# Two transformer blocks: attention scores as three float32r products of high and low halves instead of one fp32 product

## The chip, the cores and the metric

The kernel is one program on one core of a Trainium2 chip. The profile shows five engines: TensorE (PE for its matmuls, PEld for its weight loads), VectorE (DVE), ScalarE (ACT), GpSimd (POOL) and SyncE (SP), which here does nothing but issue DMAs. The metric is device time in microseconds (us) from the first to the last instruction, as the median of several runs. The profile and the trace come from one profiled execution; durations of single instructions below are from it.

## The reference

Two blocks (layers 0 and 1), each of them self-attention, cross-attention and a gated feed-forward, on x of 4 batches x 512 tokens x 320 features, with a context of 4 x 1601 x 192:

```python
def _attn(x, ctx, wq, wk, wv, wo, bo, heads):
    b, n, _ = x.shape
    j = ctx.shape[1]
    dh = wq.shape[1] // heads
    scale = dh ** (-0.5)
    q = (x @ wq).reshape(b, n, heads, dh).transpose(0, 2, 1, 3)
    k = (ctx @ wk).reshape(b, j, heads, dh).transpose(0, 2, 1, 3)
    v = (ctx @ wv).reshape(b, j, heads, dh).transpose(0, 2, 1, 3)
    sim = jnp.einsum('bhid,bhjd->bhij', q, k) * scale
    a = jax.nn.softmax(sim, axis=-1)
    out = jnp.einsum('bhij,bhjd->bhid', a, v)
    out = out.transpose(0, 2, 1, 3).reshape(b, n, heads * dh)
    return out @ wo + bo
h1 = _ln(x, n1_g, n1_b)
x = _attn(h1, h1, q1, k1, v1, o1_w, o1_b, heads) + x
h2 = _ln(x, n2_g, n2_b)
x = _attn(h2, context, q2, k2, v2, o2_w, o2_b, heads) + x
h3 = _ln(x, n3_g, n3_b)
proj = h3 @ ff_w1 + ff_b1
a, g = jnp.split(proj, 2, axis=-1)
ff = a * jax.nn.gelu(g, approximate=False) @ ff_w2 + ff_b2
return ff + x
```

There are 20 heads of 16 features. Everything is fp32.

## The kernel before

**Units.** The work is a list of units (class `Unit`, line 271). An attention unit is one layer, one batch and one group of four heads; there are five groups, so 20 self units, then 20 cross units, then 4 feed-forward units, and all of it again for layer 1. A self unit has 512 keys in `nch` = 4 chunks of 128, a cross unit 1601 keys in 13 chunks, the last of them with 65. Each of the four heads has its own 32 rows ("slot") of the tiles `q` and `kT`: 16 rows of features and one row that carries minus the row maximum (in `q`) against ones (in `kT`), the others zero.

**A chunk.** `main` (line 1068) goes over the chunks c of a unit. For a chunk it emits two rounds (`round_of`, line 1062) and a value product. A round is two score products (`score`, line 1072: keys by queries, 128 x 512 into one bank of `ps_st`), for heads 0 and 1 or for heads 2 and 3, and, from the iterator `pair` that `give` hands out, the score products for the maxima of the other two heads of a later unit (`full_two`, line 903: queries by keys, into a double bank of `ps_m`). Thus all four slots have a matmul in every round. After the matmuls come the exponentials (ACT, line 1083, into a tile of the pool `prs`) and one maximum over 128 x 2 x 512 (DVE, line 922). The value product of the chunk before follows (`values`, line 1090, four matmuls into `ps_st`), is copied by ACT into a tile `vo` of `prs` (line 1113), and added to `o` by POOL (line 1114). PSUM has four single banks for scores, values and projections (`ps_st`) and two double banks for maxima (`ps_m`).

**Maxima come first.** The score products of a unit need the maxima of its rows, so these run a unit or two ahead. `max_pairs` (line 886) makes two queues of maxima: one for heads 2 and 3, one for heads 0 and 1, each with 4 entries in a self unit and 13 in a cross unit (12 of full width and one for the last 65 keys). `give` (line 1329) hands out one entry for each round if the coming unit is `at_hand` (line 1303: its queries and keys have been in place for at least three rounds); and when the unit's start comes near (`rest == 1`, line 1344) it makes whatever is left into extra rounds without scores, which take one entry of each queue: four heads, two reductions. After a unit's last maxima, two chunks before the unit ends, `max_end` (line 966) transposes the maxima on DVE and moves them into the rows of `q` by eight DMAs on SP.

**The planner.** All else (normalisation, queries and keys, values, the output projection) waits in chains (`chains`, line 329) with costs and due times. `steps` (line 398), called once for each chunk, runs those that are due, and lets the chain "slots" run one entry for each call (`clock["slots"]`). `queries` and `keys` (lines 693, 719) project, copy the bank by ACT to a stage, and let POOL write the stage into the slots (`to_slots`, line 632). `keys_of_context` (line 747), for cross units, has four entries in "slots" instead, each of which moves one head's rows by three DMAs (`piece`, line 767); after the last one `kwhen` is set, on which `at_hand` looks.

All instructions of an engine run in the order in which this program emits them. The two lines that the text below returns to most:

```python
return not (v.q is None or v.kwhen is None) and clock["round"] >= max(v.qwhen, v.kwhen) + 3
clock["slots"] -= name == "slots"
```

## Time and profile before

| what | value |
|---|---|
| median of 3 runs (lowest to highest) | 3195.73 us (3195.3 to 3197.33) |
| the profiled execution: its span | 3195.3 us |
| PE busy | 3163.1 us (99%), granted clock 0.998 on the mean |
| DVE busy | 2069.2 us (65%) |
| ACT busy | 1972.4 us (62%) |
| POOL busy | 1204.1 us (38%) |
| first to last chunk of self units, layer 0 and layer 1 | 369.0 and 370.5 us (79 chunks each) |
| the 19 cross units behind them | 888.4 and 877.9 us (247 chunks each) |

The span of the profiled execution lies within 0.02% of the median, so it is used as the time before. The last two rows are differences between the copies of the value products (lines 1108 and 1113) in the trace, of which there is one for each chunk. Busy time is the union of an engine's or a group's instructions. A group of the list of lines names its source line, engine, operation, output<-inputs and shapes, how many there were, the busy time, the mean of one in ns, and the idle time of the engine before them with what ended it. An fp32 matmul leaves two records in the trace, each with a weight load of its own.

### The profile page before, as it was taken

How to read it: one execution, taken by the hardware profiler on the slowest of the kernel's cores; microseconds unless marked ns; L12 is line 12 of the kernel's file. 1: busy time of each engine (PE TensorE's matmuls, PEld its weight loads, DVE VectorE, ACT ScalarE, POOL GpSimd, SP SyncE). 2: the span in 40 equal slices, each digit the busy share in tenths (PEclk: the TensorE clock that was granted, in tenths of full speed). 3: DMA queues.
4: the chain of work that ended last, by engine and by line, in shares of the span. 5: the costliest groups of instructions: out<-in, count | busy, mean ns of one | idle time of the engine just before them, and what ended most of it. 6: DMA issues, size and time to landing. Idle time of an engine off the chain costs nothing. (4 is left out here: it accounts for less than half of the span.)

```text
span 3195.3 us, 81370 instructions
## 1 busy us (share of the span) xinstructions
PE 3163.1 (99%) x33970; PEld 1466.6 (46%) x33970; DVE 2069.2 (65%) x2662; ACT 1972.4 (62%) x3951; POOL 1204.1 (38%) x1617
## 2 busy tenths in 40 slices
PE   9999999999999999999999999999999999999999
PEld 4444444444444444355444444444444444443555
DVE  7787777778678677422247777777777777773221
ACT  4666577777777777611147665777778777785110
POOL 5555334443443443301135553344434444432000
PEclk9999999999999999999999999999999999999999
DMA  2220011100100100100012100010010010001000
GB/s 67 56 70 17 14 26 39 33 21 19 33 21 20 33 16 11 39 6 0 1 30 61 34 14 14 22 28 16 16 32 10 16 33 9 16 11 37 9 11 15
DMA packets 104851, 77.84 MB, mean 24 GB/s; under 512 B 42908, under 2 KB 95012, under 8 KB 104484
## 3 DMA queue, kind: packets, MB, share of 16 engines
q1 hardware_dynamic: 104400, 72.63, 9.3%
q8 instruction: 268, 4.39, 0.6%
q14 instruction: 99, 0.81, 0.1%
q0 software_dynamic: 64, 0.00, 0.0%
q10 hardware_dynamic: 20, 0.00, 0.0%
HBM read 33.04 MB, written 7.93 MB: 13 GB/s over the span
## 5 line engine op out<-in xcount | busy, mean ns | idle before, releaser
L1083 ACT ACTIVATE pr<-st 128x512 f32<-128x512 f32 (+1 forms) x2720 | 1408.6, 602 | 420.7 <-PE sps L906 360.4
L1077 PE MATMUL st<-q,kT 32*128 32x512 f32 (+1 forms) x5440 | 1362.6, 614 | 2.6 <-DVE nmax L922 1.7
L922 DVE TENSOR_REDUCE pm<-sps 128x2 f32<-128x1024 f32 (+1 forms) x974 | 1134.4, 1203 | 268.9 <-PE sps L906 262.4
L906 PE MATMUL sps<-kT,q 32*128 32x512 f32 x5120 | 1275.7, 621 | 14.2 <-DVE nmax L922 9.8
L1114 POOL TENSOR_TENSOR o<-o,vo 128x512 f32<-128x512 f32 x576 | 734.5, 1275 | 1375.8 <-ACT vo L1113 1200.7
L1077 PEld LDWEIGHTS st<-q,kT 32*128 32x128 f32 (+1 forms) x5440 | 503.8, 181 | 517.4 <-ACT pr L1083 291.1
L1097 PE MATMUL av<-pr,vals 128*32 128x512 f32 (+1 forms) x5440 | 729.3, 605 | 0.3
L922 DVE TENSOR_REDUCE nmax<-sps 128x2 f32<-128x1024 f32 (+1 forms) x338 | 378.5, 1160 | 151.7 <-PE sps L906 149.1
L906 PEld LDWEIGHTS sps<-kT,q 32*128 32x128 f32 x5120 | 406.1, 183 | 125.8 <-issue 80.6
L1113 ACT COPY vo<-av 128x512 f32<-128x512 f32 x576 | 339.8, 590 | 45.2 <-PE av L1097 41.1
L1097 PEld LDWEIGHTS av<-pr,vals 128*32 128x32 f32 (+1 forms) x5440 | 110.0, 108 | 493.4 <-ACT pr L1083 480.2
L1199 PE MATMUL fps<-hT,w 128*128 128x512 f32 x640 | 286.1, 600 | 1.0 <-DVE kT L1223 0.5
L1222 ACT ACTIVATE gl<-fps,b 128x512 f32<-128x512 f32 x80 | 50.7, 684 | 371.0 <-PE fps L1212 268.0
L647 POOL TENSOR_SCALAR q<-qst,keep,zero 64x128 f32<-64x128 f32 (+1 forms) x476 | 232.3, 488 | 58.9 <-ACT qst L711 25.5
L1199 PEld LDWEIGHTS fps<-hT,w 128*128 128x128 f32 x640 | 119.2, 191 | 152.1 <-issue 146.9
L699 PE MATMUL qps<-hT,wq 112*32 112x128 f32 (+3 forms) x2880 | 126.8, 310 | 0.5 <-DVE pm L922 0.5
L1024 PEld LDWEIGHTS ops<-wo,aT 112*32 112x32 f32 (+1 forms) x3072 | 98.4, 110 | 62.2 <-issue 32.5
L1223 DVE SCALAR_TENSOR_TENSOR hid<-fps,b,gl 128x512 f32<-128x512 f32 x48 | 33.8, 746 | 143.0 <-ACT gl L1222 143.0
L438 POOL TENSOR_SCALAR root<-root 128x4 f32<-128x4 f32 x23 | 5.3, 230 | 315.5 <-DVE root L432 314.8
L1024 PE MATMUL ops<-wo,aT 112*32 112x160 f32 (+1 forms) x3072 | 123.9, 299 | 0.2
L699 PEld LDWEIGHTS qps<-hT,wq 112*32 112x32 f32 (+1 forms) x2880 | 86.7, 110 | 79.3 <-issue 38.8
L1260 DVE TENSOR_TENSOR x<-yps,x 128x320 f32<-128x320 f32 x32 | 15.7, 492 | 148.5 <-PE yps L1253 148.5
(88 smaller groups left out, 2255.7 us busy)
## 6 DMA issues: line engine op xcount, KB each, us to landing
kT<-kst SPq DMA_DIRECT2D x320, 48.0 KB
aT<-o SPq DMA_DIRECT2D x320, 32.0 KB
q<-turned SPq DMA_DIRECT2D x636, 1.0 KB
w<-in_L_xattn_ff_w_dram SPq DMA_DIRECT2D x20, 256.0 KB
ctxT<-ctxT SPq DMA_DIRECT2D x24, 208.0 KB
ctxT<-ctxT SPq DMA_DIRECT2D x12, 416.0 KB
ctxin<-in_ctx_dram SPq DMA_DIRECT2D x24, 192.0 KB
w<-in_L_xattn_ff_w_dram SPq DMA_DIRECT2D x20, 160.0 KB
```

The costliest lines, as they stand in the source:

```text
L647: nc.gpsimd.tensor_scalar(to, stage[rows, :w], keep[b][rows], more[rows], ALU.mult, ALU.add)
L699: nc.tensor.matmul(ps[to, :w], lhsT=wq[:n, k, gs], rhs=first.hT[:n, k, at[i] : at[i] + w], start=(k == 0), stop=(k == 2),)
L906: nc.tensor.matmul(ps, lhsT=u.q[j * SLOT : (j + 1) * SLOT, t * P : (t + 1) * P], rhs=u.kT[j * SLOT : (j + 1) * SLOT, u.k0 + s * 512 : u.k0 ...
L922: nc.vector.tensor_reduce(to[:, j : j + n], part, AX.X, ALU.max, negate=(ns == 1))
L1024: nc.tensor.matmul(ps[f : f + m, : D // 2], lhsT=aT[:n, k, t * P + f : t * P + f + m], rhs=wo[:n, k, cols], start=(k == 0), stop=(k == 2),)
L1077: nc.tensor.matmul(st[:r, :], lhsT=u.kT[rows, u.k0 + u.cols[c] : u.k0 + u.cols[c] + r], rhs=u.q[rows, :], start=True, stop=True)
L1083: nc.scalar.activation(p[:r], st[:r], AF.Exp)
L1097: nc.tensor.matmul(ps[i * SLOT : (i + 1) * SLOT, :], lhsT=columns_of[:r, head : head + SLOT], rhs=pr.pop((c, j))[:r, :], start=True, stop= ...
L1113: nc.scalar.copy(vo, ps)
L1114: nc.gpsimd.tensor_tensor(u.o, u.o, vo, ALU.add)
L1199: nc.tensor.matmul(ps, lhsT=w1[:, k, i * FF + c * P : i * FF + (c + 1) * P], rhs=u.hT[:, k, :], start=ahead and k == 0, stop=not ahead and ...
L1222: nc.scalar.activation(gl, pss[1], AF.Gelu, bias=b1[:, NHC + c : NHC + c + 1])
```

## The change

A score is computed from exact sums. Queries and keys are each written as high + low, where high is the value rounded by a write with type float32r and low is the rest. A head's 32 rows of `kT` now hold, for each of 16 features, a high row and a low row; `q` has two halves side by side, the high one and the low one, each with every feature's row twice. A score for a maximum is two float32r matmuls (the high half of q, then the low half, against the same keys); a score for the softmax is these two and a third one of two rows, minus the maximum's high and low part (`mrow`) against ones.

What moves with it:

- `round_of` emits the passes of all products of a round interleaved: first pass of each, second pass of each, third pass.
- The split is done on a stage by POOL, two instructions (`split`); the rows then go to `q` and `kT` by DMAs on SP: for a self unit four for the queries and four for the keys, for a cross unit twice four and six. Each of these DMAs is an entry of the chain "slots", of which `steps` still runs one for each chunk; the marks `qwhen` and `kwhen` are set by the last entry of their group. When a stage is needed again (`stages`, `empty`) or a unit is needed at once (`at_once`), the entries left in a group are run there; their places in the chain stay, and do nothing when their turn comes.
- `max_end` splits the maxima (two more DVE instructions) and writes them by eight DMAs to `mrow`, a tile of its own.
- The pool `prs` has 8 tiles instead of 9, `oturn` one instead of two; wq2 and the stage of the cross keys lie in the room of w2, wv2 in that of w1, the context's input in that of w1r; so w1r and w2 are loaded with w1, in the last cross unit; the last four hidden tiles of the feed-forward are taken from `prs`. The tiles of blanks and their DMAs are gone.

```diff
-    prs = ctx.enter_context(tc.tile_pool(name="prs", bufs=9))
+    prs = ctx.enter_context(tc.tile_pool(name="prs", bufs=8))
...
-    qbuf = [const.tile([P, N], F32, name=f"q{i}") for i in range(4)]
+    qbuf = [const.tile([P, 2, N], F32, name=f"q{i}") for i in range(4)]
+    mrows = [const.tile([P, N], F32, name=f"m{i}") for i in range(2)]
...
-    def to_slots(t, c0, stage, w, i, with_ones, direct=None):
...
+    def split(x, high):
+
+        eng = nc.vector if start["on"] else nc.gpsimd
+        eng.tensor_scalar(high.bitcast(F32R), x, 1.0, None, ALU.mult)
+        eng.tensor_tensor(x, x, high, ALU.subtract)
...
+    groups = {"stage": deque(), "kstage": deque()}
+
+    def empty(kind, left):
+
+        while len(groups[kind]) > left:
+            g = groups[kind].popleft()
+            while g:
+                g.popleft()()
+
+    def stages(kind="stage"):
+        empty(kind, kind == "stage")
+        if kind == "kstage":
+            return [*kstage, None]
+        t = two.tile([P, 2, N // 2], F32, tag="stage", name="stage")
+        return [t[:, e] for e in range(2)] + [t]
+
+    def slots_soon(u, fs, name, kind="stage"):
+
+        fs = list(fs)
+        done = fs.pop()
+
+        def last():
+            done()
+            setattr(u, name, -9 if start["on"] else clock["round"])
+
+        group = deque(fs + [last])
+        groups[kind].append(group)
+        u.slots.append(group)
+        if start["on"]:
+            empty(kind, 0)
+        for _ in tuple(group):
+            add("slots", 0.0, lambda: group and group.popleft()(), clock["round"] + 3, yes, ready_at(clock["round"] + 2))
+
+    def ready_at(r):
+        return lambda: clock["slots"] > 0 and clock["round"] >= r
...
+            high, low, both = stages()
+            nc.scalar.mul(low[:, :w], ps[:, :w], DH**-0.5)
+            split(low[:, :w], high[:, :w])
+
+            def move(s, i):
+                queue = (nc.sync, nc.scalar)[s] if start["on"] else nc.sync
+                queue.dma_start(
+                    out=u.qbuf.rearrange("(r s) e n -> s r e n", s=2)[s][:, :, at[i] : at[i] + w],
+                    in_=both[i * GD : (i + 1) * GD, :, :w],
+                )
+
+            slots_soon(
+                u, [lambda s=s, i=i: move(s, i) for i in range(2) for s in range(2)],
+                "qwhen" if part == parts - 1 else "qpart",
+            )
...
+            slots_soon(u, [lambda e=e, i=i: move(e, i) for e in range(2) for i in range(3)], "kwhen", "kstage")
...
+        def passes(heads, outs, queries, keys):
+
+            def one_pass(e):
+                for j, out in zip(heads, outs):
+                    rows = slice(j * SLOT, (j + 1) * SLOT)
+                    nc.tensor.matmul(
+                        out,
+                        lhsT=u.q[rows, e, queries].bitcast(F32R),
+                        rhs=u.kT[rows, keys].bitcast(F32R),
+                        start=(e == 0),
+                        stop=(e == 1),
+                    )
+
+            return [lambda e=e: one_pass(e) for e in range(2)]
...
+        nc.vector.tensor_scalar(both[:, :n].bitcast(F32R), u.nm, 1.0, None, ALU.mult)
+        nc.vector.tensor_tensor(both[:, n:], u.nm, both[:, :n], ALU.subtract)
+        nc.vector.transpose(turned, both)
+        to = u.mrow.rearrange("(j s) (t i r) -> i s j t r", s=SLOT, t=NQ, r=SLOT)
+        for i in range(P // SLOT):
+            for e in range(2):
+                rows = slice(i * SLOT + e * n, i * SLOT + (e + 1) * n)
+                queue = (nc.sync, nc.scalar)[e] if start["on"] else nc.sync
+                queue.dma_start(out=to[i, e], in_=turned[rows, :])
...
     def round_of(scores, maxima):
 
-        then = [f() for f in scores] + [f() for f in maxima]
-        for f in then:
-            f()
+        todo = [f() for f in scores] + [f() for f in maxima]
+        for i in range(max((len(passes) for passes, _ in todo), default=0)):
+            for passes, _ in todo:
+                if i < len(passes):
+                    passes[i]()
+        for _, then in todo:
+            then()
...
-            nc.tensor.matmul(
-                st[:r, :], lhsT=u.kT[rows, u.k0 + u.cols[c] : u.k0 + u.cols[c] + r], rhs=u.q[rows, :], start=True, stop=True
-            )
+            keys = u.kT[rows, u.k0 + u.cols[c] : u.k0 + u.cols[c] + r].bitcast(F32R)
+            two_rows = slice(j * SLOT, j * SLOT + 2)
+
+            def product(e):
+                nc.tensor.matmul(st[:r, :], lhsT=keys, rhs=u.q[rows, e, :].bitcast(F32R), start=(e == 0), stop=False)
+
+            def less_maximum():
+                nc.tensor.matmul(
+                    st[:r, :],
+                    lhsT=units_of[two_rows, :r].bitcast(F32R),
+                    rhs=u.mrow[two_rows, :].bitcast(F32R),
+                    start=False,
+                    stop=True,
+                )
...
-        return not (v.q is None or v.kwhen is None) and clock["round"] >= max(v.qwhen, v.kwhen) + 3
+        return not (v.qwhen is None or v.kwhen is None) and clock["round"] >= max(v.qwhen, v.kwhen) + 3
...
-        while v.kslots:
-            v.kslots.popleft()()
+        for group in v.slots:
+            while group:
+                group.popleft()()
```

## Prediction

> **What bounds the kernel now.** The page first: PE is busy 99% of the span, and the four groups that a score costs are the largest of their engines.
>
> ```profile
> span 3195.3 us, 81370 instructions
> PE 3163.1 (99%) x33970; PEld 1466.6 (46%) x33970; DVE 2069.2 (65%) x2662; ACT 1972.4 (62%) x3951; POOL 1204.1 (38%) x1617
> ...
> L1083 ACT ACTIVATE pr<-st 128x512 f32<-128x512 f32 (+1 forms) x2720 | 1408.6, 602 | 420.7 <-PE sps L906 360.4
> L1077 PE MATMUL st<-q,kT 32*128 32x512 f32 (+1 forms) x5440 | 1362.6, 614 | 2.6 <-DVE nmax L922 1.7
> L922 DVE TENSOR_REDUCE pm<-sps 128x2 f32<-128x1024 f32 (+1 forms) x974 | 1134.4, 1203 | 268.9 <-PE sps L906 262.4
> L906 PE MATMUL sps<-kT,q 32*128 32x512 f32 x5120 | 1275.7, 621 | 14.2 <-DVE nmax L922 9.8
> ```
>
> ACT and DVE wait for PE (420.7 and 268.9 us), PE for nobody. Next, one chunk in the timeline of cross units (start, length, engine and line):
>
> ```profile
> 1002.78 0.70 PE L1077 MATMUL st<-q,kT 32*128 32x512 f32 x2
> 1002.79 0.70 PE L906 MATMUL sps<-kT,q 32*128 32x512 f32 x2
> 1002.97 0.59 ACT L1113 COPY vo<-av 128x512 f32<-128x512 f32 x1
> ...
> 1003.75 0.59 PE L1077 MATMUL st<-q,kT 32*128 32x512 f32 x2
> ...
> 1003.93 2.06 ACT L1083 ACTIVATE pr<-st 128x512 f32<-128x512 f32 x4 [0.38 <-PE sps L906]
> 1004.04 2.36 DVE L922 TENSOR_REDUCE pm<-sps 128x2 f32<-128x1024 f32 x2 [0.57 <-PE sps L906]
> ...
> 1004.71 1.07 PE L1097 MATMUL av<-pr,vals 128*32 128x512 f32 x8
> ```
>
> Four heads run side by side (starts 10 ns apart), records follow each other every 0.43 us, two to a product. The two rounds take 1004.71 - 1002.78 = 1.93, the value product another 0.98 (to the next round in a chunk without projections): **PE 2.92 us for a chunk**. **ACT needs 2.45**: four exponentials in 2.06 less 0.60 for the last makes 0.49 from one to the next, times five with the copy. **DVE needs 2.34**: two maxima, 1.17 apart. So PE may gain 0.47 us for a chunk before ACT ends it, and only while DVE gets its two maxima in every chunk. The third view, busy time by stage (self and cross units of layer 0, then of layer 1; PE, weight loads, DVE, ACT, POOL):
>
> ```profile
> 43.40:412.40 369.00, 361.42 (x4490) 165.35 (x4498) 285.71 (x393) 237.21 (x483) 182.96 (x279) 1.00 0.16 41
> 412.40:1300.80 888.40, 884.81 (x10858) 402.41 (x10842) 656.98 (x762) 677.12 (x1368) 373.08 (x423) 1.00 0.10 25
> 1639.40:2009.90 370.50, 363.05 (x4536) 165.90 (x4536) 277.58 (x365) 237.80 (x484) 180.15 (x266) 1.00 0.13 32
> 2009.90:2887.70 877.80, 876.84 (x10852) 397.43 (x10836) 644.09 (x720) 675.33 (x1365) 372.68 (x423) 1.00 0.09 20
> ```
>
> These 2505.7 us (652 chunks) are where the change acts; DVE and ACT are at three quarters in them, so whether three engines still work at the same time decides.
>
> **The order that the change makes.** No trace shows it, but the listing of both programs' instructions in program order does. Before, 1192 of the 1360 rounds carry two maxima beside two scores. After, 545 do; 763 rounds are scores alone (the 26 chunks of the last unit before each feed-forward have none in either), and the maxima come in about 380 extra rounds of four heads, in bunches. Two self units look like this (number of matmuls; stm is the third pass; each line a chunk):
>
> ```
> qps12 kps12 st4 stm2 st4 stm2 av4          (the same, with vps12, on three more lines)
> qps12 kps12 st4 stm2 st4 stm2 av4
> vps12 st4 stm2 st4 stm2 sps8 av4
> vps12 sps8 vps12 sps40 st4 stm2 st4 stm2 av4
> st2 sps2 st2 sps2 stm2 st2 sps2 st2 sps2 stm2 av4
> ```
>
> The cause is the chain "slots". It runs one entry for each chunk, but a self unit adds 8 entries for its 4 chunks and a cross unit 14 for its 13, and an entry whose group was emptied by force keeps its place: counted while the program is written, 18 wait at the fifth unit, 73 at the fifteenth, 80 to 116 in the cross stages. So `qwhen` and `kwhen` are set by force, late; `at_hand` says no, and `give` makes up for it when the start of the unit is near. Cross units alternate: one chunk after another paired, then some nine without maxima and a bunch of up to 14 rounds.
>
> **The sum.** For each chunk I add up each engine's work and let the chunk cost the largest of the three. PE: rounds and value product as above, and the projections listed in that chunk by their stretches in the timeline (queries 1.35 in self, 0.80 a half in cross; keys 1.40 and 2.46; values 0.70 and 1.50; output 0.93; transposes 0.97). On the kernel before this gives 358 + 895 + 357 + 892 = 2502 us against 2505.7 measured.
>
> After, a chunk's two rounds are five passes for each row slot, as slots alternate between three and two. A float32r pass of 512 columns is in no row. Ends: a quarter of a product (0.86 / 4 = 0.215) and a whole record (0.43). I take 0.22, nearest to the one pass that the diff describes: PE 5 x 0.22 + 0.98 = 2.08. An extra round costs PE 0.53 (two passes and 0.1) and DVE 2.45: one double maximum of 1.17 and two single ones of 0.64 (23.0 us for 36). A round like it exists before; PE waited 1.28 us for DVE to get to it:
>
> ```profile
> 364.53 2.32 DVE L922 TENSOR_REDUCE nmax<-sps 128x2 f32<-128x1024 f32 x2
> ...
> 365.77 1.14 PE L906 MATMUL sps<-kT,q 32*128 32x512 f32 x8 [1.28 <-DVE nmax L922]
> ```
>
> The unpaired self chunk above then costs 2.45 (ACT), the one with queries and keys 2.08 + 2.75 = 4.83 (PE), the bunch 6 x 2.45 = 14.7 (DVE). All chunks: 399 + 945 + 402 + 940 = 2687, **+185**. Two double banks and four single ones let neighbours share about one chunk of work; with the largest taken over pairs of chunks it is 2620, **+118**, which I use.
>
> What the chunk sums leave out:
> - DVE's other work. The stages show 1864 us, the sums hold 1591; 273 us (normalisation, the end of a unit, 2.3 us each) hid under PE. Chunks that DVE bounds make 37% of the new sum: **+100** (ends 0 and 273).
> - The maxima's way to the first score. In a cross unit two chunks lie between the last maxima and the next unit, 2 x 2.5 + 0.44 = 5.4 us to the third pass. The way: 1.2 to 2.45 behind on DVE after a bunch, 0.8 for four small DVE instructions (two of them new, 0.2 each like the transpose's 0.21), then eight issues and a landing:
>
> ```profile
> L977 SPq DMA_DIRECT2D q<-turned x636: 495/500/701, 29.2 to 2882.8; - x159
> ...
> DMA to landing us min/median/max: 1.8/1.9/2.0
> ```
>
> The last issue starts 4.34 us after the transpose, so 6.2: 8.2 to 9.5 in all, 2.8 to 4.1 too late, while PE and all behind it stand. ACT's store covers one to two. 40 units: 0 to 164, **+70**. Before, the maxima were ready earlier and PE waited 0.2 us for these DMAs in all.
> - The clock. Around 803 us the granted clock is down (0.72 on the mean of six us, and keys take 3.9 us instead of 2.46), after PE had stood only 1.55 us for DVE:
>
> ```profile
> 801.28 3.90 PE L755 MATMUL kps<-ctxT,w 32*64 32x224 f32 x94 [1.55 <-DVE ctxT L594]
> ...
> 800.00:806.00 6.00, 4.72 (x102) 3.50 (x106) 2.18 (x4) 0.59 (x2) 1.01 (x1) 0.72 0.08 19
> ```
>
> In a bunch PE stands 1.9 of 2.45 us. The half clock is hidden there, but the chunk behind pays up to 2 x 2.08 - 2.45 = 1.7; some 40 bunches: 0 to 70, **+35**. The Trainium skill ("TensorE: Matmul & The Clock Gate", HAM oscillation) says that only PE-idle gaps above about 3.4 us bring the clock down. By it this term would be 0; the row has a shorter gap, and I go by the row.
> - POOL. With 8 tiles in `prs` each chunk's fourth exponential waits for POOL's addition of an earlier `vo` (1.28 us, against 1.5 of ACT work before it: hidden). In front of it may stand the split of cross keys, 896 columns twice: from 128 and 256 columns (0.45, 0.56) and from 320 and 512 (0.89, 1.28) 1.1 + 2.0 = 3.2 us. 40 of them: 0 to 128; most falls behind the keys' own 2.46 on PE, **+20**.
>
> Free: the new DMAs on SP (8 to 14 of about 0.6 us for each unit, data ready long before), the shared rooms for weights (17 loads from the start of the last cross unit, about 30 us before w2 is read), the feed-forward (its matmuls stay fp32). If a load is late there, it is some us twice. The start has one more DMA trip for queries and keys, and no DMAs of blanks any more: +2.
>
> 3195 + 118 + 100 + 70 + 35 + 20 + 2 = **3540 us**. The profiled span equals the median within 0.02%.
>
> The same skill page (Back-to-back issue gap) gives 216 ns for one pass of 512 columns; an estimate by it is the sum above.
>
> **Rivals.**
> - *Faster: the engines even out.* If each ran ahead of the others by five chunks, the sum would be 2386, -116: 3080. For it: PE's own sum falls from 2498 to 2133. It decides from four chunks on (three still give 2543, +41). Against it: six PSUM tiles hold one chunk.
> - *The pass is no quarter.* At 0.43 a pass, PE has 3.13 for a chunk, the chunks sum to 3165, +663: 3860 without the other terms. If the four slots did not run side by side, ten passes a round would give about 4700. Nothing in the trace speaks for either; float32r is in no row.
> - *No change:* gain and bunches cancel, 3190 to 3202.
>
> **How the numbers follow.** Forecast 0.81 with its own range 3320 to 3800, faster 0.10, longer pass 0.07, no change 0.02 (0.2%, 6.4 us, is about what this measurement can tell). The terms' ends: 41 (three chunks) to 185 for the first, and 0 to 635 for the others, which do not all come in full together. 3300 to 3800 leaves 0.19 out. Slower: 0.81 + 0.07 = 0.88.
>
> **What would show it.** Right: PE busy well below 90%, with waits for ACT at st and for DVE at sps; chunks without maxima about 2.5 us long; bunches where DVE is full and ACT stands; the third pass waiting for the DMAs to `mrow` once per cross unit; clock 0.5 near bunches. Wrong: passes 0.43 apart; a self stage under 370 us, which would mean that chunks even out; or no wait at the third pass.

## The result and the profile after

The changed kernel takes 4311.75 us (4301.94 to 4314.49) against 3196.45 us: the ratio is 1.348, 95% interval 1.346 to 1.350. The direction was forecast, the size was not: 3540 was the forecast and 3800 the end of its range. The profiled execution has a span of 4311.9 us. Its page, then its busy time by stage (the four stages of self and cross units that were shown of before, same columns):

```profile
PE 3968.4 (92%) x36690; PEld 2023.4 (47%) x36690; DVE 2101.6 (49%) x3203; ACT 1986.5 (46%) x3949; POOL 1261.4 (29%) x1369
...
PEclk7777877789888889699987778778797688896999
...
L1104 ACT ACTIVATE pr<-st 128x512 f32<-128x512 f32 (+1 forms) x2720 | 1420.3, 601 | 984.8 <-PE st L1094 904.0
L927 DVE TENSOR_REDUCE pm<-sps 128x2 f32<-128x1024 f32 (+1 forms) x1203 | 1137.1, 1000 | 532.3 <-PE sps L906 300.8
...
L1094 PE MATMUL st<-m,units 2*128 2x512 f32 (+1 forms) x2720 | 738.4, 455 | 14.3 <-DMA m<-turned 14.2
```

```profile
52.00:635.30 583.30, 503.94 (x4934) 254.27 (x4938) 290.32 (x497) 239.81 (x486) 168.60 (x209) 0.77 0.21 45
635.30:1848.30 1213.00, 1136.85 (x11718) 582.84 (x11714) 667.63 (x927) 681.37 (x1367) 422.79 (x386) 0.82 0.14 33
2189.30:2778.50 589.20, 507.79 (x4980) 256.93 (x4976) 281.30 (x469) 240.12 (x487) 165.69 (x196) 0.78 0.19 40
2778.50:4005.10 1226.60, 1141.09 (x11724) 584.33 (x11718) 655.83 (x883) 682.59 (x1364) 422.45 (x386) 0.80 0.13 28
```

The stages went from 369.0, 888.4, 370.5 and 877.8 us to these, +1106 in all, and the feed-forward stayed (310.2 and 278.3 us). DVE and ACT do about the work that they did, and wait for about twice as long (in the lines L1104 and L927). The granted clock is the new thing: 0.77 to 0.82 in these stages. The trace's clock records have PE at half clock for 1495 us, in 136 stretches, against 12.6 us in 4 before.

Three readings of the trace. First a bunch in a self unit (start, length, engine and line):

```profile
282.70 13.98 DVE L927 TENSOR_REDUCE nmax<-sps 128x2 f32<-128x1024 f32 x18
...
286.24 7.06 PE L906 MATMUL sps<-kT,q 32*128 32x512 f32 x24 [0.40 <-DVE nmax L927]
293.81 1.81 PE L1091 MATMUL st<-q,kT 32*128 32x512 f32 x4 [0.51 <-DVE nmax L927]
295.01 1.04 PE L1094 MATMUL st<-m,units 2*128 2x512 f32 x2
295.67 1.08 ACT L1104 ACTIVATE pr<-st 128x512 f32<-128x512 f32 x2 [12.48 <-PE st L1094]
```

Six extra rounds take DVE 13.98 us, 2.33 each. The chunk's own scores come behind them, at half clock, and ACT has stood for 12.48 us: the chunk's interval is 19.25 us, where the prediction had 14.7. Second, an earlier self unit, where queries and keys are projected:

```profile
142.81 2.68 SPq L710 DMA_DIRECT2D q<-stage  x4
145.58 2.47 SPq L742 DMA_DIRECT2D kT<-stage  x4
147.50 0.38 ACT L705 ACTIVATE stage<-qps 128x256 f32<-128x256 f32 x1 [8.78 <-DMA q<-stage]
147.93 0.28 PEld L1091 LDWEIGHTS st<-q,kT 32*128 32x128 f32 x1 [6.88 <-ACT stage L705]
147.93 0.79 PE L1091 MATMUL st<-q,kT 32*128 32x512 f32 x1 [6.43 <-ACT stage L705]
```

```profile
ACT stage L705 <- DMA q<-stage: 113.7, 19, 14.9
PE st L1091 <- ACT stage L705: 76.7, 18, 12.5
```

The DMAs of an earlier unit, kept in the chain "slots", still have to read the stage when the next unit's queries want it. `empty` issues them then and there, and ACT's copy stands until they have landed: 8.78 us, with PE behind it for 6.43. The second fence is the list of waits (total, times, longest). Third, a chunk at half clock in a cross unit:

```profile
752.61 1.31 PE L1091 MATMUL st<-q,kT 32*128 32x512 f32 x4
...
753.61 0.74 PE L1094 MATMUL st<-m,units 2*128 2x512 f32 x2
753.94 1.56 PE L1091 MATMUL st<-q,kT 32*128 32x512 f32 x4
...
754.96 0.96 PE L1094 MATMUL st<-m,units 2*128 2x512 f32 x2
...
755.85 1.94 PE L1118 MATMUL av<-pr,vals 128*32 128x512 f32 x8
```

The value product has 1.94 us here and 1.07 at full clock. Of some 125 score-only chunks without a projection in cross units, those wholly at full clock have a median of about 2.79 us and those wholly at half clock 4.21.

### The profile page after: what moved, and what is told of

Its sections match the earlier page's. It is cut to its first block, busy times and chain, and to the rows that moved or that the text cites. A ratio compares the mean times of both kernels' runs of the same rounds, so it can differ in the third digit from the quotient of the medians.

```text
span 4311.9 us, 88046 instructions
## 1 busy us (share of the span) xinstructions
PE 3968.4 (92%) x36690; PEld 2023.4 (47%) x36690; DVE 2101.6 (49%) x3203; ACT 1986.5 (46%) x3949; POOL 1261.4 (29%) x1369
## 3 DMA queue, kind: packets, MB, share of 16 engines
q1 hardware_dynamic: 211368, 138.32, 14.2%
## 4 chain that ended last, share of the span: by engine, by line
PE 65%; DVE 18%; SPq 5%; ACT 4%; POOL 3%; issue 3%; DMA 2%; ACTq 0%; POOLq 0%; DVEq 0%
PE av L1118 16%; PE st L1091 16%; DVE pm L927 10%; PE fps L1218 7%; PE sps L906 6%; DVE nmax L927 5%; PE st L1094 5%; PE yps L1274 4%; ACT pr L1104 3%; PE kps L759 3%; PE ops L1030 2%; SPq L986 2%; PE qps L697 2%; PE fps L1231 2%; PE vps L849 2%
## 5 line engine op out<-in xcount | busy, mean ns | idle before, releaser
L1104 ACT ACTIVATE pr<-st 128x512 f32<-128x512 f32 (+1 forms) x2720 | 1420.3, 601 | 984.8 <-PE st L1094 904.0
L927 DVE TENSOR_REDUCE pm<-sps 128x2 f32<-128x1024 f32 (+1 forms) x1203 | 1137.1, 1000 | 532.3 <-PE sps L906 300.8
L1135 POOL TENSOR_TENSOR o<-o,vo 128x512 f32<-128x512 f32 x576 | 737.3, 1280 | 2217.0 <-ACT vo L1134 2203.3
L1091 PE MATMUL st<-q,kT 32*128 32x512 f32 (+1 forms) x5440 | 1179.0, 515 | 205.0 <-ACT stage L705 76.7
L906 PE MATMUL sps<-kT,q 32*128 32x512 f32 (+1 forms) x6400 | 1038.1, 492 | 74.7 <-DVE pm L927 31.2
L1118 PE MATMUL av<-pr,vals 128*32 128x512 f32 (+1 forms) x5440 | 917.0, 748 | 29.6 <-ACT pr L1104 26.3
L1094 PE MATMUL st<-m,units 2*128 2x512 f32 (+1 forms) x2720 | 738.4, 455 | 14.3 <-DMA m<-turned 14.2
L906 PEld LDWEIGHTS sps<-kT,q 32*128 32x128 f32 x6400 | 521.0, 225 | 358.4 <-DVE pm L927 174.7
L927 DVE TENSOR_REDUCE nmax<-sps 128x1 f32<-128x512 f32 (+1 forms) x458 | 380.5, 893 | 399.6 <-PE sps L906 397.9
L1094 PEld LDWEIGHTS st<-m,units 2*128 2x128 f32 (+1 forms) x2720 | 418.5, 218 | 78.4 <-issue 13.8
L1274 PE MATMUL yps<-w,hid 128*128 128x320 f32 x640 | 175.4, 434 | 0.0
L604 POOL TENSOR_SCALAR stage<-stage 128x128 fp32r<-128x128 f32 (+1 forms) x155 | 106.7, 688 | 187.7 <-ACT stage L705 113.5
L1274 PEld LDWEIGHTS yps<-w,hid 128*128 128x128 f32 x640 | 120.6, 190 | 55.8 <-issue 6.8
```

The lines of the kernel that those rows point to most:

```text
L604: eng.tensor_scalar(high.bitcast(F32R), x, 1.0, None, ALU.mult)
L906: nc.tensor.matmul(out, lhsT=u.q[rows, e, queries].bitcast(F32R), rhs=u.kT[rows, keys].bitcast(F32R), start=(e == 0), stop=(e == 1),)
L927: nc.vector.tensor_reduce(to[:, j : j + n], part, AX.X, ALU.max, negate=(ns == 1))
L1091: nc.tensor.matmul(st[:r, :], lhsT=keys, rhs=u.q[rows, e, :].bitcast(F32R), start=(e == 0), stop=False)
L1094: nc.tensor.matmul(st[:r, :], lhsT=units_of[two_rows, :r].bitcast(F32R), rhs=u.mrow[two_rows, :].bitcast(F32R), start=False, stop=True,)
L1104: nc.scalar.activation(p[:r], st[:r], AF.Exp)
```

## The experiments

Three theories: ORDER (bunched maxima cost the time), CLOCK (a PE that is no longer full loses its clock), STAGE (the held-back DMAs stop ACT). A fourth, RING, came up on the way. "Paired" are rounds of scores with a pair of maxima, "extra" the rounds without scores, each worth two pairs; both are counted in program order, maxima of full width only, of which there are 1280 pairs. In the trace an extra round shows as two maxima that DVE takes from single banks (128x1<-128x512): 64 in the kernel before, 762 in the changed one, 644 in before_late16, 954 in before_late24. "Half" is the time at half clock in the profiled run.

| run | paired, extra | us | ratio to before (95%) | half, us |
|---|---|---|---|---|
| before | 1216, 32 | 3195 to 3197 | | 13 |
| changed | 522, 379 | 4311.8 | 1.348 (1.346 to 1.350) | 1495 |
| moves_now | 522, 379 | 4124.9 | 1.291 (1.288 to 1.293) | 1231 |
| fill1 | 522, 379 | 4353.8 | 1.362 (1.357 to 1.367) | 1251 |
| fillbunch | 522, 379 | 4553.3 | 1.425 (1.422 to 1.428) | 1070 |
| slots8 | 1149, 65.5 | 3230.7 | 1.012 (1.010 to 1.014) | 177 |
| moves_first | 1216, 32 | 3365.6 | 1.054 (1.052 to 1.056) | 341 |
| mf5 | 1149, 65.5 | 3221.5 | 1.008 (1.006 to 1.010) | 176 |
| before_late16 | 628, 321 | 3920.2 | 1.227 (1.224 to 1.229) | 239 |
| before_late24 | 340, 466 | 4262.2 | 1.334 (1.331 to 1.336) | 385 |
| nomax4, nomax6 | none | 3051.5, 2792.5 | one run each | 185, 137 |
| slots8_acc | 1149, 65.5 | 3888.9 | 1.219 (1.215 to 1.223) | 500 |
| before_acc | as before | 3756.6 | 1.175 (1.173 to 1.178) | 9 |
| mf5_maxfirst | as mf5 | 3235.4 | 1.012 (1.010 to 1.014) | 190 |
| mf5_lastlast | as mf5 | 3232.6 | 1.011 (1.010 to 1.013) | 190 |
| mf4_lastlast | 1175, 52.5 | 3240.8 | 1.015 (1.013 to 1.017) | 175 |
| mf5_pool | as mf5 | 3208.4 | 1.004 (1.003 to 1.006) | 174 |
| mf5_early | 1115, 82.5 | 3214.9 | 1.006 (1.004 to 1.007) | 161 |

**slots8**: one number, which sets the order.

```diff
-        clock["lights"], clock["slots"] = lights, 1
+        clock["lights"], clock["slots"] = lights, 8
```

> The changed kernel, but a call of steps may run eight entries of the chain slots instead of one, so no backlog forms: the DMAs of queries and keys go out on time, qwhen and kwhen are set early, and by the listing 1140 rounds carry a pair of maxima (516 before this edit) and about 50 extra rounds remain (365). The chunk sums by the prediction's own model fall from 2634-2699 to 2063-2122 us. Theory ORDER (the bunches are the cause, and the half clock follows from them): 2750 to 3050 us, half clock under 150 us of the run, faster than the kernel before. Theory CLOCK (a PE that has passes of a quarter's length is no longer full, and that alone brings the clock down, in whatever order): 3200 us or more, half clock still over 600 us, paired chunks 3.3 us or more on the mean against 2.45 in the sum. Theory STAGE (most of the loss is ACT waiting for the DMAs that read its stage): the waits of ACT for the stage go here too, so between the two, 3000 to 3400.

3230.7 us: 1081 of the 1116 us are gone, and 1318 us of half clock with them, though PE has the same short passes. So the chain's one entry a chunk is the cause of nearly all of the loss, and most of the half clock goes with it. This run alone does not part the order from the late DMAs, as it mends both (it lies in STAGE's range too); moves_now does. ORDER's own number, 2750 to 3050, was missed: in good order the change gains nothing.

**moves_now**: the DMAs go out at the split, the marks stay where the chain sets them.

```diff
-        done = fs.pop()
+        for f in fs:
+            f()
+        fs = [lambda: None] * (len(fs) - 1)
...
-            done()
+            if kind == "kstage":
+                units[u.i - u.g].made["k"] += 1
```

> The changed kernel, but the DMAs of queries and keys are issued as soon as their rows are split; the entries in the chain slots stay and only set qwhen, kwhen and the count of keys, at the same rounds as before. So the order of the matmuls is the changed kernel's (516 paired rounds), and only the late DMAs, which ACT's next copy into the stage waits for, are gone. STAGE: the waits of ACT for the stage (113.7 us in 19 of the listed ones) and what PE loses behind them go, self stages 583 to 440 us or less, total 3950 us or less. ORDER and CLOCK: the total stays within 4130 to 4320, as the stage waits are worth their own length at most; the half clock stays above 1300 us.

4124.9 us, -187: just past the lower end of what ORDER allowed, far from STAGE's 3950; the half clock, 1231 us, is under the 1300 expected. The waits of ACT's copy for the DMAs that read its stage are no longer in the list, the 38 chunks of self units in which queries are projected fall from 8.71 to 5.74 us on the mean, and the last chunks of self units from 8.47 to 5.66. STAGE is real and worth 187 us, with the half clock that goes along.

**fill1** and **fillbunch**: redundant passes, beside every score, and three times each maximum's product in the extra rounds.

```diff
+            def filler():
+                nc.tensor.matmul(st[:r, :], lhsT=keys, rhs=u.q[rows, 0, :].bitcast(F32R), start=True, stop=True)
+
-            return [lambda: product(0), lambda: product(1), less_maximum], exponential
+            return [filler, lambda: product(0), lambda: product(1), less_maximum], exponential
```

```diff
+        if not scores:
+            todo = [(passes * 3, then) for passes, then in todo]
```

> The changed kernel, but every score product gets one more pass, the first pass done twice, whose first result is thrown away: 2720 more matmuls, which keep PE busy and change nothing else; the order of everything else is the same. By the model PE's work in a score-only chunk goes from 1.61+0.98 to 1.84+0.98 = 2.8 us at full clock, over ACT's 2.45. CLOCK: PE is full in the score-only chunks again, the clock stays up there, they go from 4.06 to 3.0 us or less, half clock from 1495 us to 900 or less, total 3900 or less, that is, more work takes less time. ORDER and STAGE: the half clock comes from the bunches and the standing for the stage, which stay; the pass adds 0 to 0.46 us to a chunk: 4300 to 4600.

> The changed kernel, its extra rounds alone with every product for the maxima made three times (six passes instead of two, some 0.9 us more of PE work in a round in which DVE has 2.45). Order and everything else the same. CLOCK as a cost of its own: PE stands less in the bunches, the half clock goes from 1495 us to under 900, and the total falls by 100 us or more, at most by the some 170 us that the bunches of the changed kernel cost more than those of before_late16 once the stage waits are taken off (1081 - 187 - 725). ORDER alone: the total stays within 60 us of 4312, whatever the clock does.

The half clock shrinks by 245 and 426 us, the time grows by 42 and 242 (fillbunch missed both of its ranges). CLOCK's claim, that more work would take less time, falls. The chunks of fill1 show why little is won: at full clock a score-only chunk rises from 2.79 to about 3.0 us with the added pass, at half clock from 4.21 to 4.64, and about half as many are left wholly at half clock. These two runs don't price the clock, as the added work has a price of its own.

**before_late24** and **before_late16**: the kernel before, with its fp32 products, in a bunched order (16 or 24 rounds).

```diff
-        return not (v.q is None or v.kwhen is None) and clock["round"] >= max(v.qwhen, v.kwhen) + 3
+        return not (v.q is None or v.kwhen is None) and clock["round"] >= max(v.qwhen, v.kwhen) + 16
```

> The kernel before (fp32 products), but at_hand says yes only 24 rounds after queries and keys are in place, instead of 3: by the listing 568 paired rounds and 336 extra rounds, nearly the changed kernel's order (516 and 365). It prices the order alone. Chunk sums 2972 to 3028 us against 2502 before. ORDER: 3670 to 3900 us, most of the changed kernel's loss without any float32r. If bunches bring the clock down by themselves: half clock over 500 us and 4000 or more. CLOCK: PE has full work between the bunches (2.92 of fp32 work a chunk), so half clock under 300 us.

> The kernel before (fp32 products) with at_hand 16 rounds late: 491 paired rounds and 389 extra rounds (the changed kernel 522 and 379). In before_late24 the count had been taken wrongly, it has 197 and 537 and cost 1067 us, which is 2.16 us for each extra round above the 43 of the kernel before. ORDER costs the same whatever the products are: 3195 + 1081 (the changed kernel less slots8) = 4200 to 4300. If an extra round costs 2.16 us wherever it stands: 3195 + 346 x 2.16 = 3940, half clock under 400 us; the 300 us that the changed kernel's bunches cost more would then go with its half clock (CLOCK as an addition to ORDER).

All counts of the kernel with fp32 products in these two texts and in that of moves_first are wrong: a paired round with an extra one right behind it was taken for extra rounds alone. The table has the right ones, and DVE's maxima from single banks agree with them. So before_late16 has 289 extra rounds more than the kernel before, where the changed kernel has 347 more: not the same dose, but near. (Ten pairs of its maxima are left out altogether, eight in before_late24.) It takes 3920.2 us, +725 with no float32r in it: 2.51 us for each extra round. before_late24 has 2.46 for each of 434, which would have made 3906 here; the 3940 of the text came near because both counts were off in the same way. The page's clock row of before_late16:

```profile
PEclk9898899999999999999998988999999999999999
```

So bunches alone cost a kernel with fp32 products some 2.5 us a round, with the clock up all but 239 us. The changed kernel has 313.5 extra rounds more than slots8; at 2.51 us they are 786 (an estimate, from before_late16). Of the 1081 us between the two, 187 are the stage, and 1081 - 187 - 786 = 108 are left. They go along with 1231 us of half clock in moves_now against 239. That they are the clock's price is argued from this and from the two chunk medians, not shown by a run.

**moves_first** and **mf5**: DMAs and marks at once, and `at_hand` 3 or 5 rounds behind them.

```diff
-        def last():
-            done()
-            setattr(u, name, -9 if start["on"] else clock["round"])
...
+        for f in fs:
+            f()
+        done()
+        setattr(u, name, -9 if start["on"] else clock["round"])
...
-        return not (v.qwhen is None or v.kwhen is None) and clock["round"] >= max(v.qwhen, v.kwhen) + 3
+        return not (v.qwhen is None or v.kwhen is None) and clock["round"] >= max(v.qwhen, v.kwhen) + 5
```

(the last two lines in mf5 alone)

> The changed kernel, but the DMAs of queries and keys are issued, and qwhen and kwhen set, in the same breath as their rows are split; nothing of them is left to the chain slots. By the listing 1216 rounds carry a pair of maxima (1194 in the kernel before) and 32 extra rounds remain (43 before, 379 in the changed kernel). ORDER alone, with the engine sums of the prediction (2038 to 2087 us for 652 chunks against 2502 before): 2780 to 2850 us. RING, the theory that eight entries a chunk suggested (3231 us, its score-only chunk 2.78 us long at full clock and not 2.45: with four single banks and five uses of them in a chunk, the last head's scores wait for ACT's copy of the value product, and this cycle of copy, round and value product sets the chunk whatever the engines' sums say): a chunk without projections gains 2.92 - 2.78 = 0.14 us at most, chunks with projections about nothing: 3110 to 3210 us, faster than the kernel before by up to 85 us. CLOCK: 3200 or more, half clock over 150 us.

> moves_first with at_hand 5 rounds after the marks instead of 3. The order of the matmuls is exactly that of slots8 (1149 paired, 65.5 extra rounds), but the DMAs go out at the split. LANDING (moves_first lost against slots8 because the maxima were given before the keys had landed, PE waiting for them for 133 us in the listed waits alone): self stages from 456 to 390-410 us, total 3200 to 3260. If the early DMAs, standing in SP's queue until POOL has split, hold up what is behind them: 3300 or more, as moves_first.

moves_first has the order of the kernel before (1216 and 32), the best of all, and loses 135 us against slots8: self stages 456 and 463 us. The group of the maxima's matmuls, of moves_first and then of mf5:

```profile
L899 PE MATMUL sps<-kT,q 32*128 32x512 f32 (+1 forms) x6400 | 1008.5, 414 | 169.6 <-DMA kT<-stage 133.5
```

```profile
L899 PE MATMUL sps<-kT,q 32*128 32x512 f32 (+1 forms) x6400 | 1004.0, 411 | 42.5 <-DMA kT<-stage 13.8
```

The maxima were given out before the keys had landed. With two rounds more between mark and use they mostly have (mf5): self stages 389 and 390, 3221.5 us, although 33.5 rounds more are extra. A mark is set when a DMA is issued, and the distance from mark to use has to cover its way through SP's queue; that was LANDING, and it held.

**nomax4** and **nomax6**: why nothing is gained in good order. Both leave out the maxima of all units but the first, so all chunks are score-only; they differ in the banks.

```diff
+        if u is not units[0]:
+            return [deque(), deque()]
...
-    ps_st = ctx.enter_context(tc.tile_pool(name="ps_st", bufs=4, space=PSUM))
-    ps_m = ctx.enter_context(tc.tile_pool(name="ps_m", bufs=2, space=PSUM))
+    ps_st = ctx.enter_context(tc.tile_pool(name="ps_st", bufs=6, space=PSUM))
+    ps_m = ctx.enter_context(tc.tile_pool(name="ps_m", bufs=1, space=PSUM))
```

> moves_first without the maxima of all units but the first: neither their products nor their reductions nor their DMAs (the row maxima of the first unit stay in their place and zeros in the other tile), so every chunk is score-only and there is no order to go wrong. Four single banks as before. Engine sums for the 652 chunks: 1960 to 2004 us, ACT the largest in a chunk without projections (2.45 against PE's 2.13). Without RING: 2.45 a chunk. RING: 2.75 to 2.8 us a chunk without projections, at full clock. CLOCK (a PE with some 80% of work loses the clock by itself): such chunks 3.5 us or more on the mean and half clock over 500 us of the run.

> nomax4 with six single banks and one double one, as no maxima need the double ones: the same instructions, but a bank that the value product used is wanted again two uses later. RING: a chunk without projections falls from 2.78 to 2.5 us (ACT's own 2.45), the stages by 100 to 200 us in all. Without RING, or if the passes or ACT alone set the chunk: no change against nomax4 within 30 us. CLOCK: the half clock does not shrink, as PE is still less full.

259 us apart, by two single banks more. The four stages gain 317 us (2368 to 2051); what lies behind them in each layer, above all the feed-forward, which uses the double bank that was given up, loses 26. The median score-only chunk of cross units takes about 2.78 us with four and 2.56 with six. A chunk of nomax4, then one of nomax6:

```profile
961.47 0.78 PE L1091 MATMUL st<-q,kT 32*128 32x512 f32 x5
961.61 0.59 ACT L1136 COPY vo<-av 128x512 f32<-128x512 f32 x1
...
962.24 0.29 PEld L1091 LDWEIGHTS st<-q,kT 32*128 32x128 f32 x3 [0.24 <-ACT vo L1136]
962.24 0.72 PE L1091 MATMUL st<-q,kT 32*128 32x512 f32 x3
...
963.13 1.07 PE L1120 MATMUL av<-pr,vals 128*32 128x512 f32 x8
```

```profile
900.38 1.06 PE L1091 MATMUL st<-q,kT 32*128 32x512 f32 x7
...
901.30 0.58 ACT L1136 COPY vo<-av 128x512 f32<-128x512 f32 x1
...
901.84 1.06 PE L1120 MATMUL av<-pr,vals 128*32 128x512 f32 x8
```

Four scores and a value product take five banks in turn, and there are four. So the last head's first pass waits until ACT has copied the value product (0.24 us; 285 such waits, 83.9 us in all); with six that wait is nearly gone (12 waits, 4.4 us). That was RING, and the wait and its end came as it said (the stages gain more than its 100 to 200 us). CLOCK falls again: all chunks are without maxima here, and the half clock stays at 185 and 137 us of the run. And a part of the missing gain is in sight: with four banks the stages take 2368 us without any maxima, where the engine sums had 1960 to 2004.

**slots8_acc** and **before_acc**: the value products of a unit summed in a PSUM bank of their own, three banks left for scores.

```diff
-            ps = ps_st.tile([P, N], F32, tag="st", name="av")
+            if c == 0:
+                u.av = ps_av.tile([P, N], F32, tag="av", name="av")
+            ps = u.av
...
-                    start=True,
-                    stop=True,
+                    start=(c == 0),
+                    stop=(c == u.nch - 1),
```

> slots8 with the value products of a unit added up in one PSUM bank of their own (start at the unit's first chunk, stop at its last): no copy vo by ACT and no addition by POOL in a chunk, three single banks for scores instead of four. Same order of the matmuls (1149 paired, 65.5 extra rounds). RING (copy of the value product, round, value product in a cycle of 2.78 us): the cycle is gone, a chunk without projections goes to PE's or DVE's own 2.2 to 2.5 us, total 2900 to 3080 us, faster than both kernels. Without RING, only ACT's work falls (by some 0.5 us a chunk), and three banks instead of four can only delay: 3180 to 3300.

> The same edit in the kernel before, fp32 products. There PE is full with 2.92 us a chunk, so neither the copy nor a ring sets the time: 3170 to 3220 us, the same as before within 1%, if the gain of slots8_acc needs the shorter passes. If the bank of its own is worth something by itself, more than 50 us faster.

Both missed: slots8_acc by 809 us against RING's range and by 589 against the other one, before_acc by 537. RING was read too narrowly, as a matter of the copy; the number of banks matters more. With three, a cross chunk of slots8_acc goes from one value product at 1001.72 us to the next at 1005.33, 3.61 us, and its second round waits for exponentials (PE's scores wait 420.7 us for them in all, against 17.2 in slots8):

```profile
1004.43 0.49 PE L1092 MATMUL st<-q,kT 32*128 32x512 f32 x1 [0.75 <-ACT pr L1105]
```

With four banks such a chunk, with maxima, has 2.80 us (the median of those of mf5 wholly at full clock). In the kernel before, where PE was 99% busy, the edit costs 561 us at a clock of 0.999, although ACT's copies and POOL's additions are gone. (In slots8_acc there are also 500 us of half clock, against 177. The edit does two things, a bank less and sums in one bank; the waits for exponentials speak for the first.)

**mf5_maxfirst, mf5_lastlast, mf4_lastlast**: is it that wait in chunks with maxima too? The first of them:

```diff
-        todo = [f() for f in scores] + [f() for f in maxima]
+        todo = [f() for f in maxima] + [f() for f in scores]
```

and of the other two, the second one with `at_hand` at 4 rounds besides:

```diff
-        todo = [f() for f in scores] + [f() for f in maxima]
+        todo = [f() for f in scores[:1]] + [f() for f in maxima] + [f() for f in scores[1:]]
```

> mf5 (3221 us), but in every round the passes for the maxima are emitted ahead of those of the scores, instead of behind. In mf5 the last head's first pass waits for ACT's copy of the value product, and the maxima's passes stand behind it in PE's order. RING through that copy: what stands behind it no longer waits, up to 0.28 us for a chunk with maxima and without projections, some 300 of them: 3140 to 3215, faster than the kernel before if over 27 us are gained. If the scores now wait for DVE to free the maxima's banks: 3230 to 3330. No change (3210 to 3230): the wait only fills what PE would stand for anyway.

> mf5, but only the second of a round's two scores is emitted behind the maxima; the first one stays ahead of them. RING: the same gain as in mf5_maxfirst without its risk at the maxima's banks, 3130 to 3205. Otherwise within 10 us of mf5's 3221.

> mf5_lastlast with at_hand 4 rounds after the marks: 1175 paired and 52.5 extra rounds instead of 1149 and 65.5. LANDING: 13 extra rounds less are worth 13 x 2.3 = 30 us, and keys that have not landed may cost as much again (moves_first, at 3 rounds, lost 67 us a self stage): within 60 us of mf5_lastlast, either side.

None gains; they are 11 to 19 us over mf5. mf5_maxfirst put one wait in the place of another, the second case of its text: PE's weight loads for the maxima wait 248.1 us for DVE (line 920; 22.2 in mf5), those for the scores 19.3 for the copy instead of 69.0. In mf5_lastlast the copy's wait falls to 25.9 without that exchange, and nothing is won. So in chunks with maxima this wait is not by itself what sets the time. What PE does there, in slots8:

```profile
906.66 0.51 PE L1091 MATMUL st<-q,kT 32*128 32x512 f32 x2
906.67 0.50 PE L906 MATMUL sps<-kT,q 32*128 32x512 f32 x2
...
907.00 0.39 PE L1091 MATMUL st<-q,kT 32*128 32x512 f32 x1
907.00 0.40 PE L906 MATMUL sps<-kT,q 32*128 32x512 f32 x2
907.01 0.62 PE L1091 MATMUL st<-q,kT 32*128 32x512 f32 x2
...
907.24 0.40 PE L1094 MATMUL st<-m,units 2*128 2x512 f32 x2
...
907.59 0.18 PEld L1091 LDWEIGHTS st<-q,kT 32*128 32x128 f32 x1 [0.29 <-ACT vo L1134]
907.60 0.50 PE L1091 MATMUL st<-q,kT 32*128 32x512 f32 x1
```

The second pass starts 0.34 us behind the first one, the third 0.24 behind the second. The line at 907.01 holds two matmuls: the second pass of one head and, at 907.24, beside the third passes, the next round's first pass of another. Only the last head's first pass stands, until the copy (907.60), and with it the maxima behind it in PE's order. In mf5_maxfirst, without that wait, two rounds still take 1.67 us in one chunk (first pass 1091.07, value product 1092.74), and their median is 1.82 against 1.84 in mf5. What sets the 2.8 us of these chunks is open: they are as long as the score-only ones of nomax4, but no run has maxima and more banks.

**mf5_pool** and **mf5_early**: the maxima's way to the first score.

```diff
-                queue = (nc.sync, nc.scalar)[e] if start["on"] else nc.sync
+                queue = (nc.sync, nc.scalar)[e] if start["on"] else (nc.sync, nc.gpsimd)[e]
```

```diff
-            if not last and c == u.nch - 3:
+            if not last and c == u.nch - (4 if u.cross else 3):
```

> mf5, but of the eight DMAs that carry a unit's maxima to mrow, the four of the low halves are issued by POOL instead of SP, so the last one starts some 2 us earlier. In mf5 the third pass waits for these DMAs 24 times, 25 us in all, and the half clock (176 us of the run) begins in several chunks right behind such a wait. If these waits bring the half clock: the waits fall below 5 us, half clock under 120 us, total 3221 to 3150-3200 us. If POOL's issue is slower, or its additions of the value products come late behind a DMA that waits for DVE: 3230 to 3300.

> mf5, but a cross unit hands its successor's maxima over one chunk earlier (the last ones, and max_end behind them, three chunks before the unit ends instead of two). The DMAs to mrow have 2.8 us more, so none of the 24 waits should be left, and what half clock follows from them goes; but by the listing 17 extra rounds more (82.5 instead of 65.5) at 2.3 us are +39. EXTRA ROUNDS decide: 3235 to 3265 us. The waits and their half clock decide: 3160 to 3215.

mf5 lost 25.1 us at the third pass to these DMAs. With four of the eight on POOL's queue 7.5 us are left of that, and the time falls to 3208.4; the half clock stays (174 us), so these waits were not what brings it. It is between the two ranges. mf5_early gives 3214.9, at the edge of its second range, with 4.9 us of these waits left: 6.6 us under mf5, whose two runs lie 8.7 apart, so this settles little. mf5_pool is the best version, 0.4% over the kernel before. No version with all its maxima beats the kernel before.

## Why the prediction was right or wrong

- *The pass is a quarter of a product:* right for the step from the second pass to the third, 0.23 us; from the first to the second it is 0.34 (medians of the 217 chunks of slots8 with maxima, without projections, wholly at full clock). The sum had 5 x 0.22 = 1.10 us for two rounds; without maxima they take 1.51 with six banks (nomax6) and 1.80 with four (nomax4), from the first pass to the value product.
- *A chunk costs the largest of three sums, 2.45 us:* this step failed, and with it fell the gain that the sum had. Neighbours are coupled through four PSUM banks: a score-only chunk takes 2.79 us, and 2.56 with six banks. With maxima it is 2.80 (median of the mf5 chunks wholly at full clock), for a reason that no run separates. Before, PE's 2.92 us filled the chunk. The model gives 2063 to 2122 us for the order of slots8, which mf5 has too; their stages take 2531 and 2521, about what the kernel before needs (2506). The half clock does not explain that: the 177 us of slots8 can have cost half of that at most, 88.
- *The order:* the cause, the count (379 of "about 380" extra rounds) and the price of a round were right: 2.33 us on DVE in a bunch against 2.45, and 2.5 us net in the runs of the kernel before. (Before, 1292 rounds carry a pair, 76 of them narrow ones, not 1192.) The +118 was the order's price, +557 in the model (2063 to 2620), less a gain of 439 (2502 to 2063). The runs have some 786 for the order and no gain but 35 us of loss, so this term alone was short by 229 + 474 = 703 of the 772 us by which the forecast missed; the larger part is the gain that isn't there.
- *The new DMAs on SP, "free: data ready long before":* this step failed too. The data were ready, but their room was wanted again: 187 us (moves_now).
- *The clock, +35:* the row was right to speak against the rule of gaps above some 3.4 us (to which the page itself does not hold as strictly as the prediction put it, see its section named at the end); the size was not. The 36 or so score-only cross chunks wholly at half clock alone cost 36 x 1.42 = 51 us; the remainder of 108 us above is the estimate for all. The half clock also runs on through chunks in which PE stands for little, which the prediction had not thought of.
- *The maxima's way, +70:* too much; 14.2 us of waiting at the third pass, in 11 waits.
- *POOL, +20:* the mechanism was right: ACT's exponentials waited 48.1 us for POOL's additions, and in 30 of the 31 waits a split of cross keys had run on POOL in the 6 us before. The split took 2.46 + 2.10 us, not 3.2. What it cost in all is not separated.
- *The start, +2:* 8.6 (first value copy at 52.0 instead of 43.4 us). *The feed-forward, 0:* right.
- *DVE's other work, +100:* not separated by any run.
- *Rivals:* "the engines even out" asked for four chunks of overlap. With four banks the engines don't even fill one chunk evenly (2.78 us in nomax4 against ACT's 2.45). "The pass is no quarter" is out by the 0.23 us.
- *The range:* with every term at its worst end the sum is 3195 + 185 + 635 = 4015, still 297 us short, so terms were missing and not only sizes wrong.
- *The signs:* PE did not fall "well below 90%" (92%; its busy time grew to 3968 us, with 1495 us at half clock), and chunks without maxima took 2.8 us or more, not 2.5; the waits at st, at sps and at the third pass, and the half clock near bunches, were there.

The account by runs: 3195 + 35 (slots8, good order) + 187 (stage, moves_now) + 894 (bunches: some 786 by the price of before_late16, 108 not separated, probably the clock) = 4311.

## What to carry to other kernels

A sum of engine times per step is a bound only while buffers let the engines run apart: count the banks that a step takes in turn against those that there are, and put that cycle beside the sums before you credit a gain to a shorter instruction. Where held-back work is released by a queue, compare what is added to it in a period with what it may release, and look at both ends: what is late when it runs late (marks, and the orders that hang on them), and who wants its source again. A mark at the issue of a DMA isn't a mark at its landing: the distance has to cover the way through the queue.

## What the runs showed of the hardware that was not expected

- Half clock comes in steps: 135 of the 136 stretches of the changed kernel are multiples of 3.41 us, the longest 88.7. It needs no long idle time: behind the first 60 us, 130 of 134 stretches have no idle time of PE above 3.4 us in the 6.8 us ahead of them. It goes on through chunks in which PE, at half speed, is full (4.20 of the 4.20 us from 752.60). The Trainium skill ("TensorE: Matmul & The Clock Gate", A second HAM failure mode: psum-queue depth-cycling) tells of a kernel whose PE idles briefly and often between groups while it cycles through PSUM banks, and whose clock swings for that. The changed kernel agrees as far as its idle times are short. nomax4, with four banks and a wait in each chunk, does not: 185 us of half clock in 3050. In these runs most of it comes where bunches and short passes meet: 1495 us, against 177 with the same passes in good order (slots8) and 239 with fp32 products in bunches (before_late16).
- The three float32r passes of a product are not evenly spaced: 0.34 us from the first to the second, 0.23 to the third. A round's third passes, on half of the row slots, and a first pass of the next round, on the others, start within 0.04 us of each other in 187 of the 217 chunks of slots8 named above.
- An edit that leaves three PSUM banks for scores instead of four costs 561 us of 3195 in a kernel whose PE was 99% busy.
